# Two edits in a four-layer image network on one core: attention denominators on TensorE, and layer 1 by row blocks

## The chip, the core and the metric

The kernel runs on one core of a Trainium2 chip. The metric is the device time of one execution in microseconds (us), the median of three runs; less is better. All data is fp32. Engines are named as the profile names them: PE is TensorE (PEld its weight loads), DVE is VectorE, ACT is ScalarE, POOL is GpSimd, SP is the engine that issues most DMA transfers.

## The reference

Input: `x` of shape (2, 128, 64, 64), two samples of 128 channels and 64 x 64 pixels. Four layers, each added to its input after a group norm (32 groups). The change touches the first two:

```python
# layer 0: attention over pixels (4 heads of 32 channels, 4096 tokens) and over channels
xn  = biasfree_ln(gn(x), ln1_w)
qkv = depthwise3x3(conv1x1(xn, w_qkv), w_dw)            # 5 x 128 channels
q1, k1, v, q2, k2 = split(qkv)                          # then heads; q and k to unit norm over tokens
out1 = softmax(q1 @ k1.T * temperature) @ v             # per head, 4096 x 4096
out2 = v @ softmax(q2.T @ k2 * temperature)             # per head, 32 x 32
x = x + conv1x1(biasfree_ln(conv1x1(out1 + out2, w_po), ln2_w), w_proj) + b_proj

# layer 1
g  = gn(x)
t1 = stack([pad(g, 6 columns each side)[..., 2*k : 2*k + w] for k in range(7)])
t2 = conv(g, w2, 1x3)
t3 = einsum('nakhw,nbhw->nakb', t1, g) / sqrt(h*w)      # seven shifted correlations, 128 x 128 each
t7 = depthwise(t2, w7, 1x5)
t8 = depthwise(g, w8, 5x5, dilation 2)
t9 = p9w * (p6w * t3)
t10 = einsum('nakb,nakhw->nbhw', t9, stack([t2 shifted by k-3 rows for k in range(7)])) / sqrt(c*7)
x = x + t8 - (t10 - t7)
```

Layer 2 filters in the Fourier domain (quaternion weights) and layer 3 is attention with 8 heads of 16 channels; neither is changed. In `t3`, shift `k` moves the columns by `2*(k-3)`; the correlation of shift `6-k` is the transpose (in a and b) of that of shift `k`.

## The kernel before

The whole image stays in SBUF as `X`, 128 channels on the partitions, 4096 pixels per sample on the free axis, cut in `NCH` = 8 chunks of `CH` = 512 pixels, each 8 rows of the image, or `NQT` = 32 blocks of 128 tokens. The layers follow each other through `X`. The engines run beside each other, each with a fixed stream of instructions; a scheduler orders each stream when the program is built, and semaphores hold an instruction until its operands are there and its buffers are free. An fp32 matmul of the program is two hardware instructions, and the profile counts these.

**Layer 0**, `_layer0`, from the start to 1979 us, takes the samples one after the other. Before the attention of a sample, `queries_keys` makes q and k: `pointwise` multiplies with a slice of `w_qkv` and ACT copies the result into a padded tile (L1087); the depthwise 3x3 is for q nine matmuls with diagonal weights `dq`, for k a chain of nine DVE operations (`depthwise`, L1099 and L1101) on row blocks of 15, 14, 14, 14 and 7 rows; `squares` (L1113) sums the squares on ACT for the norms. `values` makes the first two row blocks of v and its transposes `vt`.

The attention, `_attn_four`, then runs 8 query blocks of 512 times 32 key blocks of 128: 256 steps a sample (a *pass*). A step is:

- scores: for each of four heads a matmul of 32 rows by 512 columns, on separate row tiles of the array, into two of three buffers of two PSUM banks (`spp`), L940
- exp on ACT, two operations of 128x1024, L950
- `multiply`, for the step before: values, four matmuls on separate column tiles (L1288), accumulated over the 32 key blocks; and the denominators. For these, DVE adds the weights of four consecutive key blocks (`SUMMED` = 4; L1307 for the first addition, L1309 for the further two), and once in four steps, one step late, four matmuls with a tile of ones sum them over the keys (`sums`, also L1288, in the profile `ps_acc<-sums,ones`). At the last key block DVE copies both results, takes the reciprocal and multiplies.

Between the steps, *side work* is issued from generators, two pieces a step for the first 32 steps and one afterwards: the rest of `values`, then `channel_attention` (depthwise chains for q2 and k2 on DVE, their squares on ACT, transposes on PE at L1227, token copies on ACT at L1233, a gram matrix on PE at L1240, a small softmax), and in the first pass `normalize` of the second sample. It is used up after step 109 of the first pass and step 99 of the second. `finish` applies the projections after each pass.

```python
for n, _ in enumerate(_attn_four(nc, pp, spp, q1, k1, multiply)):
    next(side, None)
    if n < 32:
        next(side, None)
```

**Layer 1**, `_layer1`, 1979 to 2390 us, is a loop over the two samples. For each: group statistics and normalized image `g` with a border of 4 (DVE, L150); column copies `gw` (POOL, L556) that PE transposes (L559) and ACT copies into `xt`; the 1x3 convolution into `t2` (PE L575, copied by ACT at L582); the correlation `t3` over 32 column pairs, in two groups of four and three shifts, that is, 512 and 384 columns (PE, L588); `t9` from it by seven DVE operations (L598); the dilated 5x5 as 25 DVE operations of 128x4096 into `X` (the *taps*, L610); and for each of 8 row blocks a *combination* on PE: 7 matmuls of `t9` with `t2` (L617) and 5 of diagonal weights `d7` for the 1x5 (L625), which DVE adds to `X` (L633). PSUM has four banks for the combinations and transposes and two for `t3`.

Of the kernel before, what the change touches and what calls it, by code (L numbers as in the profile page):

```python
# [18 lines left out]
CH = 512  # L19
# [129 lines left out]
def _normalized(nc, out, x, mean, rstd):  # L149
    nc.vector.tensor_scalar(out, x, mean, rstd, ALU.subtract, ALU.mult)  # L150
# [357 lines left out]
def _layer1(ctx, tc, X, a, cst, eps5):  # L508
    nc = tc.nc
    one = ctx.enter_context(tc.tile_pool(name="l1_one", bufs=1))  # L510
    two = ctx.enter_context(tc.tile_pool(name="l1_two", bufs=2))
    psp = ctx.enter_context(tc.tile_pool(name="l1_ps", bufs=4, space=PSUM))
    pcp = ctx.enter_context(tc.tile_pool(name="l1_pc", bufs=1, space=PSUM))
    ident = cst["ident"]

    def bank():
        return psp.tile([128, CH], F32, tag="bank", name="ps_bank")
# [15 lines left out]
        nc.vector.tensor_scalar_mul(d7[:, s, :], ident, w7[:, s : s + 1])  # L533

    GP, TW = W + 8, W + 4
    for b in range(B):
        x = X[:, b, :]
        xi = x.rearrange("p (h w) -> p h w", w=W)
        mean, rstd = _group_stats(nc, two, bank, x, cst, eps5)
        g = two.tile([128, H + 8, GP], F32, name="g")  # L540
        nc.gpsimd.memset(g[:, 0:4, :], 0.0)
        nc.gpsimd.memset(g[:, H + 4 : H + 8, :], 0.0)
        nc.gpsimd.memset(g[:, 4 : H + 4, 0:4], 0.0)
        nc.gpsimd.memset(g[:, 4 : H + 4, W + 4 : W + 8], 0.0)
        for c in range(NCH):
            r = slice(c * ROWS, (c + 1) * ROWS)
            _normalized(nc, g[:, 4 + c * ROWS : 4 + (c + 1) * ROWS, 4 : W + 4], xi[:, r, :], mean, rstd)


        xt = two.tile([128, 32 + 6, C], F32, name="xt")  # L550
        nc.gpsimd.memset(xt[:, 0:3, :], 0.0)
        nc.gpsimd.memset(xt[:, 35:38, :], 0.0)
        for u in range(0, 32, 4):
            gw = two.tile([128, 8, H], F32, name="gw")
            w0 = 4 + 2 * u
            nc.gpsimd.tensor_copy(gw, g[:, 4 : H + 4, w0 : w0 + 8].rearrange("p h w -> p w h"))  # L556
            pt = bank()
            for i in range(4):
                nc.tensor.transpose(  # L559
                    pt[:, i * 128 : (i + 1) * 128],  # L560
                    gw[:, 2 * i : 2 * i + 2, :].rearrange("p w h -> p (w h)"),
                    ident,
                )
            nc.scalar.copy(xt[:, 3 + u : 7 + u, :].rearrange("p u c -> p (u c)"), pt)

        t2 = two.tile([128, H + 6, TW], F32, name="t2")
        nc.gpsimd.memset(t2[:, 0:3, :], 0.0)
        nc.gpsimd.memset(t2[:, H + 3 : H + 6, :], 0.0)
        nc.gpsimd.memset(t2[:, 3 : H + 3, 0:2], 0.0)
        nc.gpsimd.memset(t2[:, 3 : H + 3, W + 2 : W + 4], 0.0)  # L570
        for c in range(NCH):
            ps = bank()
            pv = ps.rearrange("p (h w) -> p h w", w=W)
            for s in range(3):
                nc.tensor.matmul(  # L575
                    pv,
                    w2[:, s, :],
                    g[:, 4 + c * ROWS : 4 + (c + 1) * ROWS, 3 + s : 3 + s + W],
                    start=(s == 0),
                    stop=(s == 2),  # L580
                )
            nc.scalar.copy(t2[:, 3 + c * ROWS : 3 + (c + 1) * ROWS, 2 : W + 2], pv)  # L582


        t3 = pcp.tile([128, 2, CH], F32, name="ps_t3")
        for lo, hi in ((0, 4), (4, 7)):
            for u in range(32):
                nc.tensor.matmul(  # L588
                    t3[:, lo // 4, : (hi - lo) * C],
                    xt[:, 3 + u, :],  # L590
                    xt[:, u + lo : u + hi, :].rearrange("p k c -> p (k c)"),
                    start=(u == 0),
                    stop=(u == 31),
                )
        t9 = two.tile([128, 7, C], F32, name="t9")
        for k in range(7):
            j = 6 - k
            nc.vector.scalar_tensor_tensor(  # L598
                t9[:, k, :],
                t3[:, j // 4, (j % 4) * C : (j % 4 + 1) * C],  # L600
                p6[:, k : k + 1],
                p9[:, k, :],
                ALU.mult,
                ALU.mult,
            )


        for s in range(25):
            i, j = 2 * (s // 5), 2 * (s % 5)
            nc.vector.scalar_tensor_tensor(  # L610
                xi, g[:, i : i + H, j : j + W], w8[:, s : s + 1], xi, ALU.mult, ALU.add
            )
        for c in range(NCH):
            ps = bank()
            pv = ps.rearrange("p (h w) -> p h w", w=W)
            for k in range(7):
                nc.tensor.matmul(  # L617
                    pv,
                    t9[:, k, :],
                    t2[:, c * ROWS + k : (c + 1) * ROWS + k, 2 : W + 2],  # L620
                    start=(k == 0),
                    stop=False,
                )
            for s in range(5):
                nc.tensor.matmul(  # L625
                    pv,
                    d7[:, s, :],
                    t2[:, 3 + c * ROWS : 3 + (c + 1) * ROWS, s : s + W],
                    start=False,
                    stop=(s == 4),  # L630
                )
            cols = slice(c * CH, (c + 1) * CH)
            nc.vector.tensor_add(x[:, cols], ps, x[:, cols])  # L633

@with_exitstack
def _layer2(ctx, tc, X, a, cst, src, eps5):
# [286 lines left out]


LIMIT = 60.0
SUMMED = 4
F32R = mybir.dt.float32r


# [71 lines left out]
def _layer0(ctx, tc, X, a, cst, eps5, worst):  # L1003
    nc = tc.nc
    one = ctx.enter_context(tc.tile_pool(name="f0_one", bufs=1))
    small = ctx.enter_context(tc.tile_pool(name="f0_small", bufs=2))
    cp = ctx.enter_context(tc.tile_pool(name="f0_ch", bufs=4))
    spp = ctx.enter_context(tc.tile_pool(name="f0_sp", bufs=3, space=PSUM))
    accp = ctx.enter_context(tc.tile_pool(name="f0_acc", bufs=2, space=PSUM))

# [8 lines left out]
    nc.vector.memset(mhalf, -0.5)  # L1019
    w_qkv = one.tile([128, 5 * C], F32, name="w_qkv")  # L1020
    nc.sync.dma_start(w_qkv, a["L0_conv_w_qkv"])
    w_po = one.tile([128, 128], F32, name="w_po")
    nc.sync.dma_start(w_po, a["L0_conv_w_po"])
    w_pr = one.tile([128, 128], F32, name="w_pr")
# [14 lines left out]


    wd = one.tile([128, 5, 9], F32, name="wd")
    with tc.tile_pool(name="f0_dw", bufs=1) as dwp:
        w_dw = dwp.tile([9, 5 * C], F32, name="w_dw")
        nc.sync.dma_start(w_dw, a["L0_conv_w_dw"])
        pw = acc()
        for g in range(5):
            nc.tensor.transpose(
                pw[:, g * 9 : g * 9 + 9], w_dw[:, g * C : (g + 1) * C], ident[:9, :9]
            )
        nc.vector.tensor_copy(wd.rearrange("p g t -> p (g t)"), pw[:, :45])  # L1050
    pp = ctx.enter_context(tc.tile_pool(name="f0_p", bufs=6))
    dq = one.tile([128, 9, C], F32, name="dq")
    for t in range(9):
        nc.vector.tensor_scalar_mul(dq[:, t, :], ident, wd[:, 0, t : t + 1])
# [225 lines left out]
        yield  # L1280

    accs = [None, None]
    parts = [None, None]

    def four(n, lhs, w, first, last):
        for j in range(4):
            rows = slice(32 * j, 32 * j + 32)
            nc.tensor.matmul(  # L1288
                accs[n][rows, :], lhs(rows), w[j // 2][:, j % 2, :], start=first, stop=last
            )  # L1290

    def multiply(qb, kt, w):


        assert kt < ready[0]
        if kt == 0:
            accs[:] = [acc(), acc()]
        four(0, lambda rows: vt[:, kt, rows], w, kt == 0, kt == NQT - 1)
        i = kt % SUMMED
        if i == 1 and kt > SUMMED:  # L1300
            sums(kt // SUMMED - 1)
        for p in range(2):
            if i == 0:
                held[p] = w[p]
            elif i == 1:
                parts[p] = pp.tile([128, 2, CH], F32, tag="sums", name="sums", bufs=4)
                nc.vector.tensor_add(parts[p], held[p], w[p])  # L1307
            else:
                nc.vector.tensor_add(parts[p], parts[p], w[p])  # L1309
        if i == SUMMED - 1:  # L1310
            whole.append(list(parts))
        if kt == NQT - 1:
            sums(kt // SUMMED)

            cols = slice(qb * CH, (qb + 1) * CH)
            u = cp.tile([128, CH], F32, tag="ch", name="u")
            nc.vector.tensor_copy(u, accs[0])
            rec = cp.tile([128, CH], F32, tag="ch", name="rec")
            nc.vector.tensor_copy(rec, accs[1])
            nc.vector.reciprocal(rec, rec)  # L1320
            nc.vector.tensor_mul(q1[:, cols], u, rec)

    held = [None, None]
    whole = []

    def sums(n):
        four(1, lambda rows: ones, whole.pop(0), n == 0, n == NQT // SUMMED - 1)

    def finish(b, w2):
        x = X[:, b, :]  # L1330
# [389 lines left out]
```

## Time and profile before

| | |
|---|---|
| median of three runs | 5445.19 us (5427.03, 5445.28, 5445.19) |
| profiled execution | 5427.03 us, span 5424.9 us |
| mean granted PE clock | 0.91 |
| busy in the span | PE 4851.9 us (89%), DVE 2362.7 (44%), ACT 3172.4 (58%), POOL 133.2 (2%) |
| layer 0 | 0 to 1979 us |
| its attention passes, first scores to last | 174.0 to 1001.7 us and 1155.7 to 1933.0 us |
| layer 1 | 1979 to 2390 us, first tap at 1995.1 |
| layers 2 and 3 | 2390 to about 3300 us, and from there to 5425 |

The profile is one execution on the chip. Its page cuts the span in 40 equal slices and gives each engine's busy share in tenths of a slice. In a timeline, a line is a run of like instructions: start in us, length in us, engine, source line, operation, the tiles written and read, shapes, how many, and in brackets the time that the engine had been idle before and the instruction that ended the wait. A matmul's end is modelled, so that lengths overlap; the distance from one start to the next is the surer measure. The windows view gives, for stretches of the span, the busy time of each engine, the clock granted to PE, and DMA.

### The profile page before, as it was taken

To read this page: it belongs to the slowest core of one execution; us is meant where nothing else is said; L and a number is where in the kernel's file an instruction comes from. 1 tells how busy PE (TensorE), PEld (TensorE's weight loads), DVE (VectorE), ACT (ScalarE), POOL (GpSimd) and SP (SyncE) were. 2 spreads that over 40 slices of the span, in tenths; PEclk is the share of its full clock that TensorE was granted. 3 is DMA by queue.
4 is the path that set the end of the run, shared out by engine and by line. 5 is a ranking of instruction groups with operands and counts; after the bars stand their busy time and mean duration, and the time that the engine had idled before them with its cause. 6 is when DMAs were issued, how large, how long until landed. Compare 5 with 4: busy or idle time off the path is not lost.

```text
span 5424.9 us, 88994 instructions
## 1 busy us (share of the span) xinstructions
PE 4851.9 (89%) x38858; PEld 2026.4 (37%) x38858; DVE 2362.7 (44%) x2680; ACT 3172.4 (58%) x3583; POOL 133.2 (2%) x118
## 2 busy tenths in 40 slices
PE   6678899967899969788888887899999999999998
PEld 3222222422222224346666666333333333333333
DVE  5777688677777886652222222422013202211001
ACT  2455488435568830001111111599999999999998
POOL 1000000000000030300000000000000000000000
PEclk9788899988899979887878885899999999999999
DMA  1000000000000000032564550000000000000000
GB/s 37 1 1 1 1 1 1 1 0 1 1 1 1 1 6 0 0 53 45 85 93 76 91 82 3 6 6 5 5 5 5 7 5 5 5 5 7 5 5 6
DMA packets 146179, 90.15 MB, mean 17 GB/s; under 512 B 8041, under 2 KB 140137, under 8 KB 145778
## 3 DMA queue, kind: packets, MB, share of 16 engines
q1 hardware_dynamic: 145778, 84.36, 9.4%
q8 instruction: 306, 5.01, 0.4%
q14 instruction: 95, 0.78, 0.0%
HBM read 75.94 MB, written 4.19 MB: 15 GB/s over the span
## 4 chain that ended last, share of the span: by engine, by line
PE 57%; ACT 2%; issue 2%; DVE 1%; POOL 1%; ACTq 0%; DVEq 0%; POOLq 0%
PE ps_acc L1546 19%; PE ps_s L1527 16%; PE ps_freq L738 5%; PE ps_bank L721 3%; PE ps_bank L710 3%; PE ps_bank L617 2%; PE ps_t L588 2%; ACT yt L718 1%; PE ps_bank L625 1%; PE ps_bank L798 1%; PE ps_bank L767 1%; PE ps_bank L575 1%; PE ps_bank L671 1%; PE ps_acc L1498 1%; PE ps_acc L1469 1%
## 5 line engine op out<-in xcount | busy, mean ns | idle before, releaser
L1537 ACT ACTIVATE weights<-ps_s 128x1024 f32<-128x1024 f32 x2048 | 1886.9, 1097 | 84.7 <-PE ps_s L1527 78.9
L950 ACT ACTIVATE weights<-ps_s 128x1024 f32<-128x1024 f32 x1024 | 994.0, 1021 | 332.8 <-PE ps_s L940 320.0
L1546 PE MATMUL ps_acc<-weights,vt 128*32 128x512 f32 x8192 | 1095.4, 607 | 0.0
L1527 PE MATMUL ps_s<-q,k 32*128 32x512 f32 x8192 | 927.5, 445 | 3.9 <-ACT weights L1537 3.1
L1527 PEld LDWEIGHTS ps_s<-q,k 32*128 32x128 f32 x8192 | 470.6, 183 | 848.9 <-ACT weights L1537 767.4
L940 PE MATMUL ps_s<-q,k 32*128 32x512 f32 x4096 | 686.5, 668 | 100.8 <-ACT weights L950 100.7
L1309 DVE TENSOR_TENSOR sums<-sums,weights 128x1024 f32<-128x1024 f32 x512 | 604.5, 1220 | 90.7 <-ACT weights L950 90.6
L1288 PE MATMUL ps_acc<-weights,vt 128*32 128x512 f32 x4096 | 593.4, 633 | 12.0 <-ACT weights L950 8.0
L1568 DVE COPY u<-ps_acc 128x512 f32<-128x512 f32 x32 | 22.1, 692 | 1005.2 <-PE ps_acc L1546 1005.2
L940 PEld LDWEIGHTS ps_s<-q,k 32*128 32x128 f32 x4096 | 214.2, 191 | 536.1 <-issue 286.6
L1307 DVE TENSOR_TENSOR sums<-weights 128x1024 f32<-128x1024 f32 x256 | 303.7, 1218 | 192.2 <-ACT weights L950 192.1
L1546 PEld LDWEIGHTS ps_acc<-weights,vt 128*32 128x32 f32 x8192 | 163.8, 108 | 380.1 <-issue 367.8
L718 ACT COPY yt<-ps_bank 128x512 f32<-128x512 f32 x128 | 74.9, 585 | 376.8 <-PE ps_bank L710 376.8
L728 DVE COPY e<-ps_bank 128x396 f32<-128x396 f32 x128 | 143.3, 1120 | 295.3 <-PE ps_bank L721 295.3
L738 PEld LDWEIGHTS ps_freq<-e,w_r 128*32 128x32 f32 x4224 | 255.8, 153 | 17.5 <-issue 11.2
L738 PE MATMUL ps_freq<-e,w_r 128*32 128x16 f32 x4224 | 259.8, 213 | 2.2 <-DVE e L728 2.2
L721 PE MATMUL ps_bank<-consts,yt 128*128 128x99 f32 x1024 | 180.1, 331 | 86.2 <-ACT yt L718 86.2
L738 PE MATMUL ps_freq<-e,w_i 128*32 128x16 f32 x4224 | 255.4, 212 | 0.0
L738 PEld LDWEIGHTS ps_freq<-e,w_i 128*32 128x32 f32 x4224 | 253.0, 157 | 2.8 <-issue 1.4
L1288 PEld LDWEIGHTS ps_acc<-weights,vt 128*32 128x32 f32 x4096 | 85.5, 110 | 431.5 <-issue 393.4
L610 DVE SCALAR_TENSOR_TENSOR X<-g,w,X 128x4096 f32<-128x4096 f32 x50 | 235.7, 4714 | 2.0
L721 PEld LDWEIGHTS ps_bank<-consts,yt 128*128 128x128 f32 x1024 | 155.6, 233 | 214.6 <-ACT yt L718 214.5
(222 smaller groups left out, 3633.5 us busy)
## 6 DMA issues: line engine op xcount, KB each, us to landing
w_r<-in_L_conv_kr_w SPq DMA_DIRECT2D x16, 528.0 KB, 12.0
w_r<-in_L_conv_kr_x SPq DMA_DIRECT2D x16, 528.0 KB
w_r<-in_L_conv_kr_y SPq DMA_DIRECT2D x16, 528.0 KB, 11.8
w_r<-in_L_conv_kr_z SPq DMA_DIRECT2D x16, 528.0 KB, 11.7
w_i<-in_L_conv_ki_w SPq DMA_DIRECT2D x16, 528.0 KB, 5.5
w_i<-in_L_conv_ki_x SPq DMA_DIRECT2D x16, 528.0 KB, 7.8
w_i<-in_L_conv_ki_y SPq DMA_DIRECT2D x16, 528.0 KB, 10.0
w_i<-in_L_conv_ki_z SPq DMA_DIRECT2D x16, 528.0 KB, 11.7
```

The lines of the kernel that those rows point to most:

```text
L610: nc.vector.scalar_tensor_tensor(xi, g[:, i : i + H, j : j + W], w8[:, s : s + 1], xi, ALU.mult, ALU.add)
L710: nc.tensor.matmul(pt, y[:, b, m, :, :].rearrange("p c w -> p (c w)"), k["perm"], start=True, stop=True,)
L721: nc.tensor.matmul(pe[:, r * 3 * FW : (r + 1) * 3 * FW], yt[:, r * 128 : (r + 1) * 128], k["fwd_w" if fh == m else "fwd_w_mirror"], start= ...
L738: nc.tensor.matmul(out.rearrange("p (x c) -> p x c", c=2), ws[n][:, :, gq * FW + fw], ef[:, :, 1 - n : 3 - n], start=(n == 0), stop=(n == 1),)
L940: nc.tensor.matmul(ps[j // 2][:, j % 2, :], k[rows, kt * 128 : (kt + 1) * 128], q[rows, qb * CH : (qb + 1) * CH], start=True, stop=True,)
L950: nc.scalar.activation(w[p], ps[p], AF.Exp)
L1288: nc.tensor.matmul(accs[n][rows, :], lhs(rows), w[j // 2][:, j % 2, :], start=first, stop=last)
L1307: nc.vector.tensor_add(parts[p], held[p], w[p])
L1309: nc.vector.tensor_add(parts[p], parts[p], w[p])
L1527: nc.tensor.matmul(ps[j // 2][:, j % 2, :], k[rows, kt * 128 : (kt + 1) * 128], q[n][rows, qb * CH : (qb + 1) * CH], start=(n == 0), stop= ...
L1537: nc.scalar.activation(w[p], ps[p], AF.Exp)
L1546: nc.tensor.matmul(ac[0][32 * j : 32 * j + 32, :], vt[:, kt, j // 2, i : i + 2, :].rearrange("p a d -> p (a d)"), w[j // 2][:, i, :], star ...
```

## The change

*Layer 0.* `SUMMED` and the sums on DVE go. `multiply` issues for every key block the four values matmuls and then four matmuls of the tile of ones with the same weights, so that the denominators are summed by PE over all keys. The load of the depthwise weights `w_dw` moves ahead of five small loads, and its tile and the weights pool `pp` are made earlier.

*Layer 1.* The loop over samples is cut into functions, whose calls for both samples are interleaved. Column copies are made by ACT. Only shifts 0 to 3 are correlated (one group of 512 columns); the other three are the transposes of shifts 2, 1 and 0, which PE makes from an SBUF copy `raw`. The middle tap of the 1x5 is added into `t9`'s middle block, so that a combination has 7 + 4 matmuls. The taps are done per row block, 25 operations of 128x512 for each of 8 blocks, and their place in the issue order is: four blocks of sample 0 after the correlation of each sample; then the combinations of sample 0; then, block by block, the taps and the combination of sample 1. PSUM has six banks for combinations and transposes and two for `t3`.

```diff
 # _layer1
-    psp = ctx.enter_context(tc.tile_pool(name="l1_ps", bufs=4, space=PSUM))
-    pcp = ctx.enter_context(tc.tile_pool(name="l1_pc", bufs=1, space=PSUM))
+    psp = ctx.enter_context(tc.tile_pool(name="l1_ps", bufs=6, space=PSUM))
+    pcp = ctx.enter_context(tc.tile_pool(name="l1_pc", bufs=2, space=PSUM))
...
-            nc.gpsimd.tensor_copy(gw, g[:, 4 : H + 4, w0 : w0 + 8].rearrange("p h w -> p w h"))
+            nc.scalar.copy(gw, g[:, 4 : H + 4, w0 : w0 + 8].rearrange("p h w -> p w h"))
...
-        t3 = pcp.tile([128, 2, CH], F32, name="ps_t3")
-        for lo, hi in ((0, 4), (4, 7)):
-            for u in range(32):
-                nc.tensor.matmul(
-                    t3[:, lo // 4, : (hi - lo) * C],
-                    xt[:, 3 + u, :],
-                    xt[:, u + lo : u + hi, :].rearrange("p k c -> p (k c)"),
-                    start=(u == 0),
-                    stop=(u == 31),
-                )
+    def correlated(xt):
+        t3 = pcp.tile([128, 4, C], F32, tag="t3", name="ps_t3")
+        for u in range(32):
+            nc.tensor.matmul(
+                t3.rearrange("p k c -> p (k c)"),
+                xt[:, 3 + u, :],
+                xt[:, u : u + 4, :].rearrange("p k c -> p (k c)"),
+                start=(u == 0),
+                stop=(u == 31),
+            )
+        raw = two.tile([128, 3, C], F32, name="raw")
+        nc.scalar.copy(raw, t3[:, :3, :])
+        swapped = bank()
+        for j in range(3):
+            nc.tensor.transpose(swapped[:, j * C : (j + 1) * C], raw[:, j, :], ident)
+        return [t3, swapped]
+
+    def taps(b, g, c):
+        xi = X[:, b, c * CH : (c + 1) * CH].rearrange("p (h w) -> p h w", w=W)
+        for s in range(25):
+            i, j = 2 * (s // 5) + c * ROWS, 2 * (s % 5)
+            nc.vector.scalar_tensor_tensor(
+                xi, g[:, i : i + ROWS, j : j + W], w8[:, s : s + 1], xi, ALU.mult, ALU.add
+            )
...
-        for s in range(25):
-            i, j = 2 * (s // 5), 2 * (s % 5)
-            nc.vector.scalar_tensor_tensor(
-                xi, g[:, i : i + H, j : j + W], w8[:, s : s + 1], xi, ALU.mult, ALU.add
-            )
...
+        nc.vector.tensor_add(t9[:, 3, :], t9[:, 3, :], d7[:, 2, :])
...
-            for s in range(5):
+        for s in (0, 1, 3, 4):
...
+    gs = [padded(b) for b in range(B)]
+    t2s, t3s, t9s = [], [], []
+    for b in range(B):
+        xt = columns(gs[b])
+        t2s.append(convolved(gs[b]))
+        t3s.append(correlated(xt))
+        for c in range(NCH // 2):
+            taps(0, gs[0], b * NCH // 2 + c)
+        t9s.append(weights(*t3s[b]))
+    for b in range(B):
+        for c in range(NCH):
+            if b:
+                taps(b, gs[b], c)
+            combined(b, t9s[b], t2s[b], c)
 # _layer0
+    pp = ctx.enter_context(tc.tile_pool(name="f0_p", bufs=6))
...
+    w_dw = one.tile([9, 5 * C], F32, name="w_dw")
+    nc.sync.dma_start(w_dw, a["L0_conv_w_dw"])
...
     def multiply(qb, kt, w):
...
-        four(0, lambda rows: vt[:, kt, rows], w, kt == 0, kt == NQT - 1)
-        i = kt % SUMMED
-        if i == 1 and kt > SUMMED:
-            sums(kt // SUMMED - 1)
-        for p in range(2):
-            if i == 0:
-                held[p] = w[p]
-            elif i == 1:
-                parts[p] = pp.tile([128, 2, CH], F32, tag="sums", name="sums", bufs=4)
-                nc.vector.tensor_add(parts[p], held[p], w[p])
-            else:
-                nc.vector.tensor_add(parts[p], parts[p], w[p])
-        if i == SUMMED - 1:
-            whole.append(list(parts))
+        for n in range(2):
+            for j in range(4):
+                rows = slice(32 * j, 32 * j + 32)
+                nc.tensor.matmul(
+                    accs[n][rows, :],
+                    ones if n else vt[:, kt, rows],
+                    w[j // 2][:, j % 2, :],
+                    start=(kt == 0),
+                    stop=(kt == NQT - 1),
+                )
         if kt == NQT - 1:
-            sums(kt // SUMMED)
```

More of the change, by code (lines that the diff above doesn't have):

```diff
@@ L535, in _layer1, with padded @@
     GP, TW = W + 8, W + 4
-    for b in range(B):
+    def padded(b):
         x = X[:, b, :]
@@ L547, in _layer1, with columns @@
             _normalized(nc, g[:, 4 + c * ROWS : 4 + (c + 1) * ROWS, 4 : W + 4], xi[:, r, :], mean, rstd)
+        return g
+    def columns(g):
         xt = two.tile([128, 32 + 6, C], F32, name="xt")
@@ L564, in _layer1, with convolved @@
             nc.scalar.copy(xt[:, 3 + u : 7 + u, :].rearrange("p u c -> p (u c)"), pt)
+        return xt
+    def convolved(g):
         t2 = two.tile([128, H + 6, TW], F32, name="t2")
@@ L582, in _layer1 @@
             nc.scalar.copy(t2[:, 3 + c * ROWS : 3 + (c + 1) * ROWS, 2 : W + 2], pv)
-        t3 = pcp.tile([128, 2, CH], F32, name="ps_t3")
-        for lo, hi in ((0, 4), (4, 7)):
-            for u in range(32):
-                nc.tensor.matmul(
-                    t3[:, lo // 4, : (hi - lo) * C],
-                    xt[:, 3 + u, :],
-                    xt[:, u + lo : u + hi, :].rearrange("p k c -> p (k c)"),
-                    start=(u == 0),
-                    stop=(u == 31),
-                )
+        return t2
@@ L595, in _layer1, with weights @@
+    def taps(b, g, c):
[5 more added lines that the diff above has]
+            )
+    def weights(t3, swapped):
         t9 = two.tile([128, 7, C], F32, name="t9")
         for k in range(7):
-            j = 6 - k
+            got = t3[:, 6 - k, :] if k > 2 else swapped[:, k * C : (k + 1) * C]
@@ L598, in _layer1 @@
             nc.vector.scalar_tensor_tensor(
-                t9[:, k, :],
[L600 to L604, printed above, removed]
-            )
-        for s in range(25):
-            i, j = 2 * (s // 5), 2 * (s % 5)
-            nc.vector.scalar_tensor_tensor(
-                xi, g[:, i : i + H, j : j + W], w8[:, s : s + 1], xi, ALU.mult, ALU.add
-            )
-        for c in range(NCH):
[L614 to L622, printed above, removed]
-                )
-            for s in range(5):
[L625 to L633, printed above, removed]
@@ new lines, in weights, with combined @@
+                t9[:, k, :], got, p6[:, k : k + 1], p9[:, k, :], ALU.mult, ALU.mult
+            )
+        nc.vector.tensor_add(t9[:, 3, :], t9[:, 3, :], d7[:, 2, :])
+        return t9
+    def combined(b, t9, t2, c):
+        ps = bank()
+        pv = ps.rearrange("p (h w) -> p h w", w=W)
+        for k in range(7):
+            nc.tensor.matmul(
+                pv,
+                t9[:, k, :],
+                t2[:, c * ROWS + k : (c + 1) * ROWS + k, 2 : W + 2],
+                start=(k == 0),
+                stop=False,
+            )
+        for s in (0, 1, 3, 4):
+            nc.tensor.matmul(
+                pv,
+                d7[:, s, :],
+                t2[:, 3 + c * ROWS : 3 + (c + 1) * ROWS, s : s + W],
+                start=False,
+                stop=(s == 4),
+            )
+        cols = slice(c * CH, (c + 1) * CH)
+        x = X[:, b, cols]
+        nc.vector.tensor_add(x, ps, x)
@@ L927 @@
 LIMIT = 60.0
-SUMMED = 4
 F32R = mybir.dt.float32r
@@ L1041, in _layer0 @@
     wd = one.tile([128, 5, 9], F32, name="wd")
[L1042 to L1051, printed above, removed]
+    pw = acc()
+    for g in range(5):
+        nc.tensor.transpose(pw[:, g * 9 : g * 9 + 9], w_dw[:, g * C : (g + 1) * C], ident[:9, :9])
+    nc.vector.tensor_copy(wd.rearrange("p g t -> p (g t)"), pw[:, :45])
     dq = one.tile([128, 9, C], F32, name="dq")
@@ L1282, in _layer0 @@
     accs = [None, None]
[L1283 to L1290, printed above, removed]
     def multiply(qb, kt, w):
@@ L1297, in multiply @@
             accs[:] = [acc(), acc()]
-        four(0, lambda rows: vt[:, kt, rows], w, kt == 0, kt == NQT - 1)
-        i = kt % SUMMED
-        if i == 1 and kt > SUMMED:
-            sums(kt // SUMMED - 1)
-        for p in range(2):
-            if i == 0:
-                held[p] = w[p]
-            elif i == 1:
-                parts[p] = pp.tile([128, 2, CH], F32, tag="sums", name="sums", bufs=4)
-                nc.vector.tensor_add(parts[p], held[p], w[p])
-            else:
-                nc.vector.tensor_add(parts[p], parts[p], w[p])
-        if i == SUMMED - 1:
-            whole.append(list(parts))
+        for n in range(2):
+            for j in range(4):
+                rows = slice(32 * j, 32 * j + 32)
+                nc.tensor.matmul(
+                    accs[n][rows, :],
[3 more added lines that the diff above has]
+                    stop=(kt == NQT - 1),
+                )
         if kt == NQT - 1:
-            sums(kt // SUMMED)
             cols = slice(qb * CH, (qb + 1) * CH)
@@ L1321, in multiply @@
             nc.vector.tensor_mul(q1[:, cols], u, rec)
[L1323 to L1327, printed above, removed]
     def finish(b, w2):
```

## The prediction

> **What bounds the kernel now.** I read the page's busy slices first (135.6 us each), then the timeline of layers 0 and 1 by engine, and last the windows view of the stretches found there.
>
> ```profile
> PE   6678899967899969788888887899999999999998
> DVE  5777688677777886652222222422013202211001
> ACT  2455488435568830001111111599999999999998
> PEclk9788899988899979887878885899999999999999
> ```
>
> Layer 0 fills slices 1 to 15, layer 1 the next three (1979 to 2390). TensorE leads in both, with dents. The windows view takes the undisturbed rest of attention pass 0, then pass 1 split where its side work ends, then layer 1:
>
> ```profile
> core 0: us, PE busy (x) PEld busy (x) DVE busy (x) ACT busy (x) POOL busy (x), PEclk, DMA share, GB/s
> 654.00:1002.00 348.00, 348.00 (x2620) 91.22 (x2620) 274.51 (x235) 282.02 (x291) 0.00 (x0) 1.00 0.00 1
> 1155.70:1561.00 405.30, 330.44 (x1989) 96.14 (x1988) 308.80 (x304) 226.08 (x250) 1.56 (x5) 0.87 0.00 1
> 1561.00:1933.00 372.00, 372.00 (x2793) 97.28 (x2792) 289.95 (x249) 300.70 (x311) 0.00 (x0) 1.00 0.00 1
> 1979.00:2390.00 411.00, 330.82 (x808) 153.72 (x808) 270.34 (x130) 20.59 (x35) 85.26 (x36) 0.87 0.01 2
> ```
>
> In the rests TensorE never pauses: they are as long as its instructions. With side work it idles 75 of 405 us. A rest, on TensorE's timeline:
>
> ```profile
> 804.16 1.07 PE L1288 MATMUL ps_acc<-weights,vt 128*32 128x512 f32 x8
> 805.15 1.20 PE L940 MATMUL ps_s<-q,k 32*128 32x512 f32 x8
> 806.28 1.06 PE L1288 MATMUL ps_acc<-weights,vt 128*32 128x512 f32 x8
> 808.46 1.06 PE L1288 MATMUL ps_acc<-weights,vt 128*32 128x512 f32 x8
> 809.34 1.04 PE L1288 MATMUL ps_acc<-sums,ones 128*32 128x512 f32 x8
> ```
>
> One attention step is a values group and a scores group, 806.28 less 804.16 = 2.12. Every fourth step also has a ones group (the denominators, on VectorE's sums): the values group then takes 809.34 less 808.46 = 0.88, ones 0.97. Bare steps average 2.13, ones steps 3.04, 32 steps 76.8, so 2.40 each. Where side work stalls:
>
> ```profile
> 277.13 1.21 DVE L1101 SCALAR_TENSOR_TENSOR qk<-pad,wd,qk 128x960 f32<-128x960 f32 x1
> 278.37 1.00 ACT L1113 ACTIVATE junk<-qk 128x960 f32<-128x960 f32 x1 [7.46 <-DVE qk L1101]
> 279.28 0.19 ACT L1113 ACTIVATION_READ_ACCUMULATOR junk<-qk 128x1 f32 x1
> 279.38 2.83 ACT L950 ACTIVATE weights<-ps_s 128x1024 f32<-128x1024 f32 x3
> 280.43 2.08 PE L940 MATMUL ps_s<-q,k 32*128 32x512 f32 x4 [6.27 <-ACT weights L950]
> ```
>
> ScalarE's square waits for VectorE's depthwise chain, the exp behind it is late, and TensorE has no score buffer. In layer 1, VectorE's timeline:
>
> ```profile
> 1995.08 82.71 DVE L610 SCALAR_TENSOR_TENSOR X<-g,w,X 128x4096 f32<-128x4096 f32 x17
> 2103.10 1.90 DVE L598 SCALAR_TENSOR_TENSOR t<-ps_t,p,p 128x128 f32<-128x128 f32 x7 [25.31 <-PE ps_t L588]
> 2104.92 36.12 DVE L610 SCALAR_TENSOR_TENSOR X<-g,w,X 128x4096 f32<-128x4096 f32 x8
> 2155.88 0.69 DVE L633 TENSOR_TENSOR X<-ps_bank,X 128x512 f32<-128x512 f32 x1 [9.71 <-PE ps_bank L625]
> ```
>
> VectorE and TensorE take turns: each sample's taps are held up by the correlation (25.31, then 29.31), and its adds come at TensorE's 10.4 a row block.
>
> **What the Trainium skill says.** "TensorE: Matmul & The Clock Gate", Part 1: after an idle window of about 3.4 us the array runs at half rate until busy that long. The trace agrees: behind the 6.27 gap the next groups take 2.08 and 1.94, not some 1.1. Its fact table calls ScalarE's and VectorE's queues strict FIFO; so stands the exp above. Part 3: matmuls on separate 32-wide tiles run together. The trace: eight hardware instructions of 512 columns in 0.88, where a full-array one takes 0.432. "SBUF — State Buffer", two separate sides: a VectorE operation with two SBUF inputs and a GpSimd operation that reads SBUF lock each other out. Here only partly: taps beside GpSimd's copies start every 4.87, others every 4.53.
>
> **The change part by part.** Layer 0, denominators. The instruction order built from the changed program has a ones group after each values group. *Removed:* VectorE's sums, 1.22 each, 2.44 a step in three of four (908 us busy in all, L1307 and L1309). *Added:* three ones groups in four steps. A step becomes 0.88 + 0.98 + 1.07 (scores start to start) = 2.93 (2.88 to 3.04 by single groups). TensorE stays the bound: two exps take 2.04, VectorE falls idle. In the rests nothing hides this:
>
> - pass 0, 145 steps: 145 x 2.93 - 348 = +77; pass 1, 155 steps: 155 x 2.93 - 372 = +82. **Rests +159.**
>
> With side work there are two opposite effects. Before, pass 1 took 777.4; 255 steps x 2.40 = 612, so side work cost 165. Pass 0: 827.7 - 612 = 216, the 51 more being the next sample's normalize. What of this 381 stays? Of a pass's share, TensorE's own side work stays: 42 (pointwise, transposes, gram). I keep waits for token copies, 12, the channel softmax chain, 11, and waits for buffers and value transposes, 6. The squares' waits remain, shorter: the new order puts the square two steps behind the pad copy (three before). The nine depthwise operations take 0.69 + 8 x 1.143 = 9.8 for 14 rows. Counting from a step's scores, the pad is ready at 5.9, the chain at 15.9, ScalarE reaches the square at 10.9 and waits 4.9, and three score buffers leave TensorE losing 4.4 (15 rows 5.4, 7 rows 2.7): 2 x 5.4 + 6 x 4.4 + 2 x 2.7 = 43 a pass. Gaps near 4 us bring half rate: about 17. Sum 131; pass 0 with normalize 181.
>
> - with side work: pass 0 110 x 2.93 + 181 = 503 against 479.7; pass 1 100 x 2.93 + 131 = 424 against 405.3. **+43. Layer 0: +202.**
>
> The depthwise weights' load (23 KB, on SP) moves ahead of five small loads; the next stage waits for the input's normalize to 60 us, so nothing, and without that cover one transfer, 2 at most.
>
> Layer 1. The tap chain becomes VectorE's uninterrupted work, with the next sample's transposes, convolution and correlation under it.
>
> - Taps: 400 of 128x512 for 50 of 128x4096. 448 elements start every 0.683, 896 every 1.143; between them 512 gives 0.75 (L1346, 128x512, 0.747): 400 x 0.75 = 300, where before they took 238. Splitting costs 62.
> - Beside them on VectorE: second normalize 3.7, statistics 0.5, t9 14 (rows L598 and two small adds), 16 adds of 0.63 = 10.1. From the first tap, as before at 1995.1, this gives 318.6, to **2313.7**; the last add ended at 2389.7. **-76**: 62 for the split against 55 of correlation waits, some 80 of waits for adds and 6 for the lighter contention.
> - TensorE under it: correlation 64 hardware instructions x 0.432 = 27.6 (448 of 896 columns remain), three 128-wide transposes and a copy 2, combination 22 x 0.434 = 9.55 for 10.4. t9 of sample 0 is ready at 2067, VectorE wants it at 2074; sample 1's at 2138, wanted 2151. The combinations, 153 from there, end at 2291, before VectorE.
> - Column copies go from POOL (5.03 each, 16) to ScalarE: not in the trace there; 0.585 (L564, contiguous) to 1.2 (L728's strided copy, 1.12 for 396). I take 0.9; 1.2 adds 5 a sample, within the 7.7 of slack. ScalarE is busy 21 of 411. POOL's queue only keeps memsets.
>
> Layer 2's weight and constant loads, issued on SP at layer 1's end, and its half-rate start move along whole. Layer 3 is untouched: 0.
>
> Sum: +202 - 76 = **+126**. The profiled execution had 5427.0 (span 5424.9), 18.2 under the median 5445.2; so 5553 against it, **5571** against the median.
>
> **Rivals.** (a) The forecast; own range 5510 to 5620: 2.88 to 3.04 a step moves it -26 to +56, taps at 0.70 to 0.80 by 20 either way, layer 1's slack overrun adds up to 15. (b) *The waits don't shorten*: side work costs all 381 again, +69, net +195: **5640**. For it: the queue order is the same kind; against: all the sums that lengthened VectorE's queue ahead of the squares are gone. (c) *VectorE's relief ends ScalarE's waits altogether*, **faster** side: only TensorE's 42, copies and softmax chain, 71 a pass, and 121 with normalize stay: 192 of 381, layer 0 +82, net +5: 5451. It decides when more than 187 of the 381 go (then net zero), and is faster by over 27 when more than 214 go; with hardly any waits but TensorE's 42 and half normalize, 136, net -50: 5395. For it: VectorE was busy 309 of 405 there, much of it sums, and squares waited on its backlog. Against: the chain of nine alone is longer than the two steps that the new order gives it. (d) The change not doing what it says: the order shows 400 taps and the ones groups, so no chance.
>
> **How the numbers follow.** A measurement tells about 0.5%, 27 us, from nothing. (a) 0.70; (b) 0.16; (c) 0.14, of which 0.05 faster by over 0.5%, 0.08 within, 0.01 slower. Slower: 0.70 + 0.16 + 0.01 = 0.87. The range runs from 5465, into (c), to 5650, past (b).
>
> **What would show it.** In the rests: steps of 2.93, TensorE fully busy, no sums on VectorE; passes of about 928 and 878. ScalarE's waits before squares of 4 to 6, not 7.5. Layer 1 near 335, VectorE busy throughout, no wait before t9. Wrong would be: stretches with side work (to steps 110 and 100) far from 503 and 424, a bare step over 3.1 (ScalarE or the clock binds), or taps far from 0.75.

## The result, and the profile after

The changed kernel took 5495.56 us in the median of four runs (5481.28 to 5499.43), the kernel before 5439.52 (5427.03 to 5445.28): ratio 1.0101, 95% interval 1.0074 to 1.0129. That is 56 us slower, where 126 were forecast: the same side, inside the range of 5465 to 5650, but below the 5510 at which the forecast's own range (a) began.

Lines of the busy slices of the page after; a slice is now 137.4 us (5494.9 / 40):

```profile
PE   6789899988899998987888888799999999999998
DVE  5532200064221004993222222422012111201001
ACT  2455366625556664101111111399999999999998
PEclk9899899998999998996888886799999999999999
```

VectorE has emptied in layer 0 (slices 1 to 15) and filled up in layer 1 (17 and 18, at 9). The windows view of a rest of pass 0, of pass 1's stretch with side work, and of layer 1 (columns as before):

```profile
677.40:1101.50 424.10, 424.10 (x3486) 105.76 (x3482) 21.70 (x16) 281.00 (x291) 0.00 (x0) 1.00 0.00 1
1254.00:1667.60 413.60, 379.21 (x2588) 106.47 (x2587) 142.04 (x155) 225.78 (x250) 1.56 (x5) 0.93 0.00 1
2168.00:2471.00 303.00, 263.53 (x654) 118.03 (x654) 299.45 (x483) 37.47 (x53) 5.44 (x20) 0.94 0.01 3
```

In the rest TensorE is still the whole of the time, now 424 us for 145 steps. TensorE's timeline in it:

```profile
804.21 1.06 PE L1319 MATMUL ps_acc<-weights,vt 128*32 128x512 f32 x8
805.09 1.04 PE L1319 MATMUL ps_acc<-weights,ones 128*32 128x512 f32 x8
806.07 1.14 PE L970 MATMUL ps_s<-q,k 32*128 32x512 f32 x8
807.14 1.06 PE L1319 MATMUL ps_acc<-weights,vt 128*32 128x512 f32 x8
```

Values 0.88, ones 0.98, scores 1.07, each from one start to the next: a step is 807.14 less 804.21 = 2.93. A square beside side work, three lines of the timeline of all engines:

```profile
264.95 1.00 ACT L1140 ACTIVATE junk<-qk 128x960 f32<-128x960 f32 x1 [6.41 <-DVE qk L1128]
265.96 2.83 ACT L980 ACTIVATE weights<-ps_s 128x1024 f32<-128x1024 f32 x3
267.01 2.08 PE L970 MATMUL ps_s<-q,k 32*128 32x512 f32 x4 [4.66 <-ACT weights L980]
```

The same chain of waits as before, 6.41 and 4.66 for 7.46 and 6.27, and the scores group behind it again takes 2.08, as it did before. VectorE in layer 1, four lines of its timeline:

```profile
2190.79 63.69 DVE L615 SCALAR_TENSOR_TENSOR X<-g,w,X 128x512 f32<-128x512 f32 x96
2254.39 0.86 DVE L623 SCALAR_TENSOR_TENSOR t<-ps_bank,p,p 128x128 f32<-128x128 f32 x3
2256.41 66.34 DVE L615 SCALAR_TENSOR_TENSOR X<-g,w,X 128x512 f32<-128x512 f32 x100
2326.82 0.69 DVE L651 TENSOR_TENSOR X<-ps_bank,X 128x512 f32<-128x512 f32 x1 [0.86 <-PE ps_bank L642]
```

No wait stands before t9 (the three operations at 2254.39), and the longest wait before an add is 1.56. But 100 taps take 66.34: 0.663 each, not 0.75.

The forecast's terms against the two profiled executions:

| | forecast | measured |
|---|---|---|
| rests of the attention passes | +159 | 424.1 - 348.0 and 453.4 - 372.0: +158 |
| stretches with side work | +43 | 502.8 - 479.7 and 413.6 - 405.3: +31 |
| layer 1 | -76 | 302.2 - 410.3: -108 |
| layers 2 and 3, unchanged | 0 | 3024.3 - 3035.1: -11 |
| sum | +126 | +70 |

The profiled execution of before lay 12.5 below the median of its four runs, that of after 1.4 above, which makes +56 of the +70. The load of the depthwise weights that moved shows nothing: the first scores start at 174.6, before at 174.0.

### The profile page after: what moved, and what is told of

Same layout as the page of the kernel before. It is cut to its first block, busy times and chain, and to the rows that moved or that the text cites. A ratio compares the mean times of both kernels' runs of the same rounds, so it can differ in the third digit from the quotient of the medians.

```text
span 5494.9 us, 93939 instructions
## 1 busy us (share of the span) xinstructions
PE 5043.9 (92%) x41776; PEld 2039.6 (37%) x41776; DVE 1513.4 (28%) x2264; ACT 3188.7 (58%) x3601; POOL 53.4 (1%) x102
## 4 chain that ended last, share of the span: by engine, by line
PE 85%; DVE 9%; ACT 4%; issue 1%; POOL 1%; DMA 0%; SPq 0%; ACTq 0%; DVEq 0%; POOLq 0%
PE ps_acc L1553 19%; PE ps_acc L1319 16%; PE ps_s L1534 15%; PE ps_s L970 9%; PE ps_freq L769 5%; PE ps_bank L752 3%; DVE qk L1128 3%; PE ps_bank L741 3%; PE ps_acc L1190 2%; DVE X L615 2%; PE ps_sp L1102 1%; ACT yt L749 1%; PE ps_bank L829 1%; PE ps_bank L798 1%; PE ps_t L596 1%
## 5 line engine op out<-in xcount | busy, mean ns | idle before, releaser
L1553 PE MATMUL ps_acc<-weights,vt 128*32 128x512 f32 x8192 | 1095.1, 607 | 0.0
L1534 PE MATMUL ps_s<-q,k 32*128 32x512 f32 x8192 | 926.5, 444 | 4.5 <-ACT weights L1544 3.6
L1534 PEld LDWEIGHTS ps_s<-q,k 32*128 32x128 f32 x8192 | 470.7, 183 | 846.9 <-ACT weights L1544 766.1
L970 PE MATMUL ps_s<-q,k 32*128 32x512 f32 x4096 | 643.9, 654 | 68.0 <-ACT weights L980 68.0
L1319 PE MATMUL ps_acc<-weights,vt 128*32 128x512 f32 x4096 | 575.0, 629 | 0.0
L1319 PE MATMUL ps_acc<-weights,ones 128*32 128x512 f32 x4096 | 570.0, 612 | 0.0
L970 PEld LDWEIGHTS ps_s<-q,k 32*128 32x128 f32 x4096 | 174.6, 187 | 498.4 <-issue 370.9
L1575 DVE COPY u<-ps_acc 128x512 f32<-128x512 f32 x32 | 22.1, 692 | 1003.8 <-PE ps_acc L1553 1003.8
L615 DVE SCALAR_TENSOR_TENSOR X<-g,w,X 128x512 f32<-128x512 f32 x400 | 266.9, 745 | 0.1
L1330 DVE COPY u<-ps_acc 128x512 f32<-128x512 f32 x16 | 11.1, 691 | 922.1 <-PE ps_acc L1319 922.1
L1319 PEld LDWEIGHTS ps_acc<-weights,ones 128*32 128x32 f32 x4096 | 138.8, 113 | 333.8 <-issue 332.5
```

Source lines behind the costliest of these rows:

```text
L615: nc.vector.scalar_tensor_tensor(xi, g[:, i : i + ROWS, j : j + W], w8[:, s : s + 1], xi, ALU.mult, ALU.add)
L970: nc.tensor.matmul(ps[j // 2][:, j % 2, :], k[rows, kt * 128 : (kt + 1) * 128], q[rows, qb * CH : (qb + 1) * CH], start=True, stop=True,)
L1319: nc.tensor.matmul(accs[n][rows, :], ones if n else vt[:, kt, rows], w[j // 2][:, j % 2, :], start=(kt == 0), stop=(kt == NQT - 1),)
L1534: nc.tensor.matmul(ps[j // 2][:, j % 2, :], k[rows, kt * 128 : (kt + 1) * 128], q[n][rows, qb * CH : (qb + 1) * CH], start=(n == 0), stop= ...
L1553: nc.tensor.matmul(ac[0][32 * j : 32 * j + 32, :], vt[:, kt, j // 2, i : i + 2, :].rearrange("p a d -> p (a d)"), w[j // 2][:, i, :], star ...
```

## The experiments

Ratios, with their 95% intervals, are to the kernel before, which ran on the same chip beside each group (medians 5427.1 for e1 to e4, 5427.2 for e5 to e8, 5433.5 for e9 to e11). Theory: layer 0 loses what TensorE's ones groups add, layer 1 gains by overlap, and the missing 32 us are the taps, which are cheaper where the scheduler alternates two row blocks. First the two halves, each alone.

```diff
 # e1: the kernel before
-_layer1 of the kernel before
+_layer1 of the changed kernel
 # e2: the kernel before
-_layer0 of the kernel before
+_layer0 of the changed kernel
```

> Layer 0 of the kernel before with layer 1 of the changed one. If the two halves are independent, layer 1 takes the 303 us that it has in the changed kernel against 411: about -108, so some 5331 against 5439. If the forecast's 0.75 us a tap was right and the changed kernel's other gain came from somewhere else (layers 2 and 3 were some 10 shorter in its profile), it is -76: 5363.

> Layer 0 of the changed kernel with layer 1 of the one before. Forecast's sum for it: +202, 5641. The profile of the changed kernel has layer 0 189 later: 5628. If layer 1's trace in the changed kernel hid a cost of layer 0, or the reverse, the two halves don't add up to the measured +56.

Measured: e1 5307.48, ratio 0.9781 (0.9748 to 0.9814), -120. e2 5625.5, ratio 1.0372 (1.0355 to 1.0390), +198. In e1's profile the time from the first tap to layer 2's statistics is 286.5, as in the changed kernel (394.5 before). e2's attention passes take 926.4 and 866.9, the changed kernel's 926.9 and 866.9. The halves add up to +78, against +56 measured in another comparison and +70 between the profiles; single runs of one kernel lie up to 38 us apart. As far as this spread can tell the halves are independent, and the change is a gain of some 110 to 120 with a loss of some 190 to 200.

**The price of a tap.** The built program shows the taps of two row blocks alternating on VectorE: block 0 tap 0, block 1 tap 0, block 0 tap 1, and so on, each waiting on the semaphore for the operation two before it. e3 makes alternation impossible:

```diff
 # taps
+        t = one.tile([128, ROWS, W], F32, tag="tap", name="tap")
...
-                xi, g[:, i : i + ROWS, j : j + W], w8[:, s : s + 1], xi, ALU.mult, ALU.add
+                xi if s == 24 else t, g[:, i : i + ROWS, j : j + W], w8[:, s : s + 1],
+                t if s else xi, ALU.mult, ALU.add
```

> The changed kernel with every block's 25 taps accumulated in one temporary tile of one buffer, so that no two blocks' taps can alternate. Theory (alternating blocks are independent of each other, so an operation starts before the one ahead of it has ended: 0.663 start to start where each lasts 0.745): a dependent chain costs 0.745 plus the 0.035 that the dependent depthwise chain shows between operations, 0.78, so 400 x 0.117 = +47: layer 1 some 350, total 5542. Rival (shape and pitch of the operands make the tap quick, not independence): 0.66 again, no change.

Measured: 5542.27, ratio 1.0212 (1.0195 to 1.0229). VectorE's timeline in e3:

```profile
2207.33 18.08 DVE L616 SCALAR_TENSOR_TENSOR tap<-g,w,tap 128x512 f32<-128x512 f32 x23
```

23 taps in 18.08: 0.787 each start to start, for the same shape and pitch that took 0.663 alternating. First tap to layer 2's statistics is 329.8, +43. The rival falls: with the same shape and pitch a tap is quick only where it does not wait for the result of the one before it. Nor is it the temporary tile that slows it: where an operation of t9 stands between two taps of e3, that one starts 0.66 after the tap ahead of it.

**The squares.** e4 takes from ScalarE what held up the exps.

```diff
 # squares, for q2 and k2 alone
-        nc.scalar.activation(junk[:, :n], t, AF.Square, accum_out=at)
+        nc.vector.tensor_mul(junk[:, :n], t, t)
+        nc.vector.tensor_reduce(at, junk[:, :n], AX.X, ALU.add)
```

> The changed kernel with the ten squares of q2 and k2 in each pass as a multiply and a reduce on VectorE, instead of one activation on ScalarE. Theory (ScalarE's square waiting for the depthwise chain is what stalls attention): TensorE's 34 us of waits for exp in a pass and some 17 of half rate behind them go: about -100, 5395. Rival (the wait passes to TensorE's own transposes of the same tile, which stand in its queue behind the same chain): -30 or less.

Measured: 5395.6, ratio 0.9948 (0.9932 to 0.9965): 100 below the changed kernel's median (some 84 by the two ratios), now under the kernel before. The passes took 856.6 and 804.8 for 926.9 and 866.9, 132 less in the profiled execution; this was 122 shorter than the changed kernel's, as the unchanged layers 2 and 3 took 11 more. Windows view of e4, pass 1's stretch with side work:

```profile
1183.20:1532.00 348.80, 343.82 (x2566) 99.65 (x2568) 162.12 (x175) 215.71 (x228) 1.56 (x5) 0.99 0.00 1
```

TensorE idles 5 of 349 us, not 34 of 414, and its clock is 0.99 for 0.93. The waits did not pass to the transposes: beside pass 0's side work TensorE waits for no depthwise chain, and the 34.0 us that it waited for exps in the changed kernel are gone. e5 does the same in e1, where VectorE also carries the sums.

> As the layer-1-alone kernel (5307), with the ten squares of q2 and k2 in each pass on VectorE. If ScalarE's square is the stall of the kernel before too, as it was of the changed one: TensorE's 75 us of idling in pass 1's side work and most of the half rate go, about -50 a pass, 5207. Rival (VectorE, which carries the sums here and was busy 309 of 405 us, gets 21 more and becomes what attention waits for: exps wait for weights buffers that the late sums still hold): -30 at most, 5277.

Measured: 5248.07, ratio 0.9683 (0.9648 to 0.9718), 59 below e1: between the two. ScalarE's waits in e5 while pass 0 has side work (total, times, longest):

```profile
ACT weights L981 <- PE ps_s L971: 113.9, 88, 11.3
ACT weights L981 <- DVE sums L1342: 42.9, 18, 7.5
```

The second line is the rival's: exps wait for weights buffers that late sums hold. In e1 they wait 2.3 for sums, and the squares 68.9 for depthwise chains. The stall has changed its cause, and its smaller part stayed: TensorE waits 51.0 for exps in e1, here 16.4 for exps and 11.3 for sums.

**What layer 1 owes to which part.** e6 is e1 with two row blocks a tap:

```diff
 # taps, and their calls for every second block
-        xi = X[:, b, c * CH : (c + 1) * CH].rearrange("p (h w) -> p h w", w=W)
+        xi = X[:, b, c * CH : (c + 2) * CH].rearrange("p (h w) -> p h w", w=W)
...
-                xi, g[:, i : i + ROWS, j : j + W], w8[:, s : s + 1], xi, ALU.mult, ALU.add
+                xi, g[:, i : i + 2 * ROWS, j : j + W], w8[:, s : s + 1], xi, ALU.mult, ALU.add
```

> As the layer-1-alone kernel, with taps of 128x1024 (two row blocks at once, 200 instead of 400). An alternating tap then starts every 1.067 + 0.13 = 1.2 us, 240 us for 265: -25 if VectorE alone sets the end. TensorE has 263 us of work in layer 1's 303, so it should come to bind: I expect -15, layer 1 from first tap to last add some 271 for 286. Rival (the wider tile leaves the last two combinations to the end, each 9.55): no gain.

Measured: 5288.95, ratio 0.9747 (0.9712 to 0.9781), 18.5 below e1, and 269.3 from the first tap, 17 less. The runs of the two overlap, so the trace is the surer sign. 20 taps take 24.00, 1.20 each, as reckoned; the last add waits 7.02 for TensorE, which now shares the bound.

```diff
 # e7: columns
-            nc.scalar.copy(gw, g[:, 4 : H + 4, w0 : w0 + 8].rearrange("p h w -> p w h"))
+            nc.gpsimd.tensor_copy(gw, g[:, 4 : H + 4, w0 : w0 + 8].rearrange("p h w -> p w h"))
 # e8: the calls
+    for b in range(B):
+        g = padded(b)
+        xt = columns(g)
+        t2 = convolved(g)
+        t9 = weights(*correlated(xt))
+        for c in range(NCH):
+            taps(b, g, c)
+        for c in range(NCH):
+            combined(b, t9, t2, c)
```

> The changed kernel with the column copies gw back on POOL. Taps beside a POOL copy cost 7% more before (4.87 for 4.53), 80 us of copies: +6. And 8 copies of 5.03 put xt of a sample at 40 us, with the convolution (21) meanwhile on TensorE: t3 of sample 0 ends perhaps 15 later, of which 12 were slack: +3. Layer 1 286 + 9 = 295. Rival (VectorE's and POOL's reads lock each other out entirely, as the Trainium skill's SBUF page has it): 80 us of copies would stop taps for 80: 366.

Measured, one run: 5526.85, and 307.9 from the first tap, 21 more than in the changed kernel, not 9 and not 80. The copies themselves and the taps (shortest, median and longest ns), then VectorE beside copies:

```profile
L560 POOL COPY gw<-g x16: 1103/1428/17217, 2187.0 to 2273.4; 128x512 f32<-128x512 f32 x16
L615 DVE SCALAR_TENSOR_TENSOR X<-g,w,X x400: 734/745/1599, 2186.9 to 2493.3; 128x512 f32<-128x512 f32 x134
```

```profile
2187.54 1.07 DVE L137 TENSOR_TENSOR gn_d<-gn_mv,gn_mean 128x1 f32<-128x1 f32 x1
2191.94 7.81 DVE L150 TENSOR_SCALAR g<-X,gn_mean,gn_rstd 128x512 f32<-128x512 f32 x8
```

A copy takes 1.1 at least. Where it meets VectorE's work the two mostly take turns: five copies beside taps last 1.54 to 1.57 and seven taps 1.59 to 1.60, a one-column VectorE operation takes 1.07 (0.14 without a copy), eight normalizations 7.81 (3.73 in the changed kernel). One copy of the sixteen got no turn while 24 taps started beside it at their usual pace, and lasted 17.2; why this one was not tried. Of the 21, 8 are lost before sample 0's t9, and the rest in longer waits for combinations, 8.84 and 2.22 among them, and in taps slowed by copies after it.

> The changed kernel's layer 1 with its parts in the order of the kernel before: a sample's columns, convolution, correlation and t9, its 8 blocks of taps, its 8 combinations, then the next sample. If row blocks are what counts (a combination's add waits only for its block's taps, combinations run beside the taps of later blocks): little is lost, sample time some 58 to t9 plus 8 x 9.55 = 135 to 145, layer 1 some 290 to 300. If the interleaving of the samples is what hides the correlation: its waits return, 25 and 29, and the second sample's combinations stand at the end: 340 or more for 286.

Measured, one run: 5532.1, and 323.0 from the first tap, 36.5 more: between the two. Its VectorE at the end of sample 0:

```profile
2321.99 3.09 DVE L651 TENSOR_TENSOR X<-ps_bank,X 128x512 f32<-128x512 f32 x5
2334.00 0.69 DVE L651 TENSOR_TENSOR X<-ps_bank,X 128x512 f32<-128x512 f32 x1 [8.92 <-PE ps_bank L642]
2343.53 0.69 DVE L651 TENSOR_TENSOR X<-ps_bank,X 128x512 f32<-128x512 f32 x1 [8.84 <-PE ps_bank L642]
```

Six combinations are ready when the taps end (one stands just before these lines), as many as PSUM has banks for them; the last two are waited for, 17.8 a sample, and the next sample's work stands behind them. The correlation is not waited for, even so: t9 follows the first tap after 57.6 us (108.0 before, with waits of 25 and 29; here 1.24). So of the 108, interleaving the samples is worth some 36 by this one run. What else changed makes up the rest: that t9 comes early, by the four shifts and ScalarE's columns (some 21 by e7) together, the row blocks, six banks for four, and 11 matmuls for 12 in a combination. Beyond e7 it was not divided.

**Which engine should sum, and where.** e9 to e11 combine e5's layer 0 with e6's layer 1, and choose the denominators' way by query block: `m` = 1 for the first three (side work), 4 later (e9); 2 and 4 (e10); 1 and 8 (e11).

```diff
 # multiply
-        i = kt % SUMMED
+        m = 1 if qb < 3 else 4
+        i = kt % m
+        if m == 1:
+            four(1, lambda rows: ones, w, kt == 0, kt == NQT - 1)
...
-        for p in range(2):
+        for p in range(2 if m > 1 else 0):
```

> Layer 0: squares of q2 and k2 on VectorE; the ones groups for every key block only in the first three of eight query blocks (where the side work is), sums of four on VectorE in the other five. Layer 1 of the changed kernel with taps of 1024 columns. If the two ways of making the denominators suit different stretches: the first 96 steps take the 333 us of the changed kernel with squares on VectorE, against 357 with sums, and the rests stay at 2.40 a step: 5248 (old layer 0 with squares moved) - 18 (wider taps) - 2 x 24 = 5182. Rival (after the squares are moved it makes no difference who sums): 5230.

> As the one above, with sums of two in the first three query blocks: TensorE has 48 ones groups less (0.80 each above a bare step: -38 a pass), VectorE 48 x 2.44 = 117 more on 162 + some: 279 in 295 us. If VectorE can bear it: -20 a pass, 5142. If its queue holds up the exps again, as with sums of four there (43 us of waits for sums): no gain or +10 a pass, 5182 to 5202.

> As the first of the three, with sums of eight in the five later query blocks. TensorE's step falls from 2.40 to 2.13 + 0.91/8 = 2.24, VectorE's sums rise to 2.44 x 7/8 = 2.13 a step with 5.4 at the end of a query block (2.30 in all): if TensorE sets the pace 2.24, if VectorE 2.30: -16 to -25 a pass over 160 steps, 5132 to 5150. Rival (VectorE at over 95% holds the weights buffers and exps wait): at or above 2.40, 5182 or more.

Measured: e9 5181.67, ratio 0.9550 (0.9522 to 0.9578); e10 5216.43, ratio 0.9606 (0.9575 to 0.9637); e11 5160.34, ratio 0.9500 (0.9472 to 0.9527). From the first scores to those of the 97th step pass 0 took 334.0 in e9, 344.9 in e10 and 358.5 in e5. e9 came out as expected. e10's gain did not come, and its passes are 17 and 13 longer than e9's, more than its bad case had: ScalarE waits 45.7 for sums there, as much as in e5. e11 is 21 below e9 and 10 above its expected range. A rest step of it takes 219.3 / 95 = 2.31, of e9 2.40. Windows view of e11, mostly a rest of pass 1:

```profile
1420.00:1794.00 374.00, 371.63 (x2712) 97.39 (x2708) 344.92 (x311) 308.27 (x321) 0.00 (x0) 1.00 0.00 1
```

TensorE is busy for all but 2 of 374 us and VectorE for 345, so TensorE still sets the pace, though 2.31 is near the 2.30 reckoned for VectorE. The 2.24 reckoned for TensorE left out the end of a query block: 32 steps of the kernel before took 76.8, and 24 of 2.13 with 8 of 3.04 make 75.4. The 1.4 between them is an estimate of that end, and with it 28 bare steps and 4 with ones give 2.29. e11 beats both kernels, by 5.0% the one before.

## Why the prediction was right and wrong

- **Rests, right.** Steps of 2.93 as reckoned from single groups; +158 for +159. Nothing hid TensorE's ones groups, and VectorE's sums, 908 us of busy time, had bound nothing there.
- **Stretches with side work, nearly right.** Pass 0's took 502.8 for 503, pass 1's 413.6 for 424. Reckoned as the forecast reckons, side work cost 301 of the 381, where 312 were forecast. ScalarE's ten waits in pass 0 sum to 52.8, 5.3 each (forecast 4 to 6). TensorE lost 34.0 to late exps in each pass, not 43, so that pass 0 came out to the microsecond is luck: its other terms were larger by as much. Rival (b), unshortened waits, and (c), none at all, both fall; e4 shows what (c) would have needed, the squares off ScalarE: -100.
- **Layer 1, wrong in size.** The failed step is the price of a tap, "between them 512 gives 0.75": measured 0.663, outside the 0.70 to 0.80 that were allowed for, and a sign of being wrong that the forecast had named. Two faults in it pull apart. The depthwise chains from which it was interpolated depend each on the one before, and the taps, alternating, do not. And the 0.683 for 448 elements is the length of an operation (684 ns in the lines view), as L1346's 0.747 is, not a distance between starts. Two runs of a chain in the kernel before:

```profile
264.05 6.24 DVE L1101 SCALAR_TENSOR_TENSOR qk<-pad,wd,qk 128x960 f32<-128x960 f32 x5
512.56 3.63 DVE L1101 SCALAR_TENSOR_TENSOR qk<-pad,wd,qk 128x448 f32<-128x448 f32 x5
```

Five operations take four distances and one length (1.22 and 0.68), so these start every 1.26 and 0.74, which gives 0.80 for 512: near the 0.787 that e3 measured for a dependent tap. So 0.75 lies between two true prices, and right distances with the dependence still taken for granted would have missed by more. A tap lasts 0.745 but the next starts after 0.663: 400 x 0.087 = 35, of which 32 show. The order of instructions by block would have told it before any run. The other terms held: t9 without a wait, combinations ahead of the taps.
- **How the miss adds up.** Of the 70 between +126 and the measured +56, layer 1 is 32, layer 0 is 13, layers 2 and 3 are 11, and 14 lie between the profiled executions and the medians.
- **The 18 us between profile and median**, carried over whole, were mostly a matter of which execution was profiled: 12.5 with a fourth run, and -1.4 after.
- **Layers 2 and 3** gave -11 between the two profiles. In the profiles of the kernels here, none of which changes them, they take 3012 to 3035 together, with no relation to the change. Why they vary was not tried.
- **Slips in the working.** The "14" of t9 reads as a number of operations: the 318.6 stated comes out with 4.3 us for them (seven took 1.90 before). +43 is +42 by its own terms. In rival (c), 187 is what may stay of the 381: for net zero 194 must go, and 221 for 27 faster. None of these changes the outcome.
- **GpSimd's lock.** "Here only partly" was a misreading. 4.87 is the mean of a run of 17 taps; singly a tap beside a copy is followed after 5.24, any other after 4.52. The copies of 5.03 can be read as short ones that waited for a tap of 4.5 to end: alone one takes 1.1. That fits what the Trainium skill says ("SBUF — State Buffer", two separate sides): one holds the port for its whole instruction and the other waits. The copy of 17.2 in e7, passed over by 24 taps, does not follow from that. VectorE loses 0.7 a copy before and 0.9 in e7, somewhat less than a copy's own 1.1; e7's rival took the copies for 5 us each, which they are not.

## What to carry to other kernels

Price a chain of in-place operations from rows whose neighbours depend on each other in the same way, by distances from start to start and not by lengths, and look in the built order at which blocks alternate. Choose by stretch which engine does a reduction: the one that idles there, and where two queues wait for each other, take the small operation at the crossing off the queue that feeds the bound. A profile's distance to the median of other runs is no property of a kernel; leave it out of the sum and put it into the range.

## What the runs showed of the hardware

- VectorE starts the next 128x512 scalar_tensor_tensor (fp32, two inputs in SBUF) 0.663 us after the one before when they are independent, and 0.787 when it reads its result; each lasts 0.745 to 0.752. The Trainium skill ("Vector Engine (DVE) Microarchitecture Reference", measured stream behaviour on trn2) has 1.0417 ns a column and some 75 ns an instruction after overlap, an estimate of 0.61 for 512; the measured 0.663 lies above it, and a dependent pair a further 0.124.
- A GpSimd copy of 128x512 that takes 1.10 us mostly took turns with such VectorE operations (1.54 to 1.57 beside a tap of 1.59), but one of sixteen lasted 17.2 beside them.
